# A four-layer graph network on one core: the seam between the LSTM and the first dense layer re-ordered

## The chip, the cores and the metric

The kernel runs on one core of a Trainium2 chip. A core has five engines, each with its own queue of instructions: PE (matrix multiply, with a weight loader shown as PEld), DVE (vector), ACT (activation functions), POOL (general SIMD) and SP (issues DMA transfers). Matmul results land in PSUM[...]. The metric is the device time of one execution in microseconds; the median of three runs is compared.

## The reference

Activations are x, [128 graphs, 64 nodes, 256 channels] in f32: 8192 tokens. Four layers follow each other, each as `x = x + layer(relu(layernorm(x)))`.

```
layer 0:  h = relu(adj @ (h @ Wg0 + bg0));  h = relu(adj @ (h @ Wg1 + bg1))
          for p in 1..4:  windows of p nodes -> LSTM over the p steps (weights of p),
                          the last hidden state replaces node p-1 of each window
layer 1:  h = A_hat @ h;  h = relu(batchnorm(h @ W1.T + b1));  batchnorm(h @ W2.T + b2)
layer 2:  a 3-way graph convolution with the diagonal, upper and lower part of adj
layer 3:  one attention head with a causal mask, then @ Wo
```

W1 is 512x256, so layer 1's first dense product makes 512 channels from 256. Its batch norm needs the mean and variance over all 8192 tokens before anything after it can go on.

## The kernel before, in words

Tokens are worked on in 16 supertiles `s` of 512 tokens. Most products use one level of Strassen: seven products in place of eight, with sums of weight blocks made in advance (`weight_sum`, four per weight, on POOL) and sums of data blocks made as they are needed. The code never lets a scheduler choose: each operation is recorded with a planned time through `at(...)`, the list is sorted by that time, and each engine gets its instructions in that order. The planned times only set the order. [...]

**Layer 0, graph part** (`graph_part`, `ROUND`): one supertile per round. Beside it POOL makes the summed LSTM weights of p = 2..4, six pieces per round (`stage`), and stores them in DRAM.

**LSTM** (`first_step`, `outer_step`): a step for one state is 52 slots of PE work. A slot is one 128x512 matmul or two 128x256 ones; each f32 matmul shows as two records in the trace, so 4 records of 128x256 or 2 of 128x512 are one slot. After the last slot comes a tail off PE: DVE adds the last banks to the gates (`chained` L1007, `take` L980), ACT applies the gates (`act` L1013), POOL computes `in_times_g` (L1023) and `plus` (L1029), with `keep` (L1026) before, ACT takes the tanh of the cell (`squash` L1032), and DVE multiplies with the output gate (`out` L1038). `n` is one of two halves of the data. In the very last step (`fin`) the POOL part goes by channel halves.

**Seam** (`begin`, `First`): while the last LSTM step runs, the first supertiles of layer 1 are prepared. For each: PE transposes the LSTM result (`turn` L666), ACT copies it out of PSUM (`turned` L670), POOL adds it to x (`added` L674), DVE takes layer norm statistics (`stats` L685, L686), POOL takes the root (`root` L692, L693), ACT normalises (`relu` L699), PE multiplies with the adjacency (`agg` L708), and ACT or DVE copies that to SBUF (`agged` L712). W1 is loaded in four transfers (`load_w1` L146) and its four sums are made on POOL (L314) in this stretch.

**First dense product** (`half`, `GATE`): supertiles go in pairs `i`, output channels in two halves `g`. One `half(i, g)` has seven products (L1290) into three banks:

```
c = (c,2)                              one product
b = (b,5) then (b,3)
a = (a,1), (a,6), (a,7), (a,4)         evicted between the steps
```

(a,1) is read by ACT (`evict` L1295) before (a,6) may add to the same bank. DVE adds the other banks to the evicted blocks (`add` L1298) and takes batch norm statistics (L1301). The data sums t1, t2, b12, t4 (`ag_sums` L1191) are made by DVE for pair 0 and by POOL for most others. At the start of this product the eight LSTM banks are closed and two new pools opened: `new_banks(gates=5, rest=3)`.

Of the kernel before, what the change touches and what calls it, by code (L numbers as in the profile page):

```python
# [14 lines left out]
P = 128  # L15
# [5 lines left out]
def kernel(ctx: ExitStack, tc: tile.TileContext, a: dict, out: bass.AP):  # L21
# [120 lines left out]
    def load_w1():  # L142
        con["w1"] = hlast.tile([P, 7, 2, P], F32, tag="w1", name="w1")
        for o in range(2):
            for c in range(2):
                nc.sync.dma_start(con["w1"][:, 2 * o + c], a["W1T"].rearrange(  # L146
                    "(c p) (g o m) -> o c p g m", c=2, p=P, o=2, m=P)[o, c])
# [182 lines left out]
    def pairs_of(p):  # L330
# [5 lines left out]
        if nblk % 2 == 0 and nw % nblk == 0:  # L336
# [8 lines left out]
              for p in range(2, NL + 1) for n, size in SUMS.items()}  # L345
    ORDER = (0, 2, 3, 1)
# [65 lines left out]
    with tc.tile_pool(name="pa", bufs=2) as pa, tc.tile_pool(name="pax", bufs=3) as pax:  # L412
# [189 lines left out]
        START = (9.01, 11, 19.01)  # L602
# [6 lines left out]
        at_piece = 3  # L609
# [38 lines left out]
    class First:  # L648
# [9 lines left out]
        def turn(self, k):  # L658
            v = self.v
            if k == 0:  # L660
                tag = "ag" if self.s == 3 else "h"
                v["h"] = pb[0].tile([P, Q, D], F32, tag=tag, name=tag)
            v["T", k] = bank(self.pool).rearrange("p (q d) -> p q d", q=2)
            for q in range(2):
                for c in range(KC):
                    nc.tensor.transpose(v["T", k][:, q, ts(c, P)], tile_rows(self.s, c, 2 * k + q), ident)  # L666

        def turned(self, k):

            nc.scalar.copy(self.v["h"][:, slice(2 * k, 2 * k + 2)], self.v["T", k])  # L670

        def added(self, k):
            v, qs = self.v, slice(2 * k, 2 * k + 2)
            nc.gpsimd.tensor_add(v["xt"][:, qs], v["xt"][:, qs], v["h"][:, qs])  # L674
# [20 lines left out]
        def relu(self, q):  # L695
            v = self.v
            if self.s == 3 and q == 0:
# [230 lines left out]
    def outer_step(t0, st, j, tags, fin):  # L928
# [105 lines left out]
        def out(n):  # L1034
            m = ("21", "22")[n]
            if last:
                for c in range(KC):
                    nc.vector.tensor_mul(x(n, c), wide(gate_(m, 0)[:, c]), wide(gate_(m, 1)[:, c]))  # L1038
# [21 lines left out]
        for c in range(KC):  # L1060
            tick((-26 if one else -38) + 0.6 * c, T1, c)
        for k, s in ((0, -35), (1, -34), (3, -33)):
            tick(s + 12 * one, inner_sum, 5, k)
# [41 lines left out]
        for c in range(KC if fin else 1):  # L1105
            c = slice(c, c + 1) if fin else slice(0, KC)
            tick(e, in_times_g, 1, c)
            tick(e, plus, 1, c)
        tick(58.5, out, 0)
        tick(e + (6.5 if last and p < NL else 4.2), squash, 1)  # L1110
        tick(e + (8.8 if last and p < NL else 6), out, 1)
        st["h_at"] = t0 + e + 6
# [68 lines left out]

    def ag_sums(i, k, engine=nc.gpsimd):
# [3 lines left out]
        if k == 0:  # L1186
            if i == 0:
                t = sums_of.tile([P, 3, 512], F32, tag="th", name="T")
                firsts[0]["t"] = [t[:, n, :] for n in range(3)]
# [3 lines left out]
    def begin(s, t_load, t_turn=None, t_stats=None, t_relu=None, t_agg=None):  # L1193
# [11 lines left out]
        def agg(c):  # L1205
            f.agg(c)
            f.agged(c, nc.vector.tensor_copy if s else nc.scalar.copy)
# [10 lines left out]
        if t_stats and s != 3:  # L1218
# [5 lines left out]
    begin(2, 7.9, 20.3, 21.4, 25.3)  # L1224
    begin(3, 17, 24.3, 25.4)
    begin(4, 21.4)
    at(t + 34.6, load_w1)
    for k in range(4):
        at(t + 48 + 0.1 * k, lambda k=k: weight_sum(con["w1"], k))
    at(t + 52.2, lambda: seam.extend(("a0", "a1", "c", "b")))  # L1230
    at(t + 68, lambda: First(3).root())
    for k in range(4):
        at(t + 57.4 + 0.1 * k, ag_sums, 0, k, nc.vector)
# [24 lines left out]
    with tc.tile_pool(name="pz", bufs=1, reuse_waits="tile") as pz:  # L1258
# [11 lines left out]
        new_banks(gates=5, rest=3)  # L1270
        GATE = 8.7
        B = GATE * (NS - 2)
# [5 lines left out]
        def half(i, g):  # L1278
            t0, r = GATE * (2 * i + g), {}
            z = {(n, o): zslot(2 * i + n, 2 * g + o) for n in range(2) for o in range(2)}  # L1280

            def product(name, j):
                new = name not in r
                if new:
                    r[name] = bank("gates")
                (b11, b21), (b12, b22) = ([firsts[2 * i + n]["ag"][:, c, :] for c in range(KC)]
                                          for n in range(2))
                t1, t2, t4 = firsts[0]["t"]
                x_ = (b11, b21, b22, t4, t1, t2, b12)[j - 1]
                nc.tensor.matmul(r[name], con["w1"][:, OF[j], g, :], x_, start=new,  # L1290
                                 stop=(name, j) in (("a", 4), ("b", 3), ("c", 2)), skip_group_check=True)

            def evict(n, o, name):
                m = 2 * g + o
                nc.scalar.activation(z[n, o], r[name], AF.Identity, bias=con["bn1"][:, 0, m : m + 1])  # L1295

            def add(n, o, name):
                nc.vector.tensor_add(z[n, o], z[n, o], r[name])  # L1298
# [5 lines left out]
            if end:  # L1304
                t0 = B + 6.02 * g
            late_a = 6.1 if g else 6.9
            for t, name, j in (((0, "c", 2), (1.72, "a", 1), (2.58, "b", 5), (3.44, "a", 6), (4.3, "b", 3),
# [3 lines left out]
                at(t0 + t, product, name, j)  # L1311
            for t, fn, n, o, name in (((2.6, evict, 0, 0, "a"), (3.3, add, 0, 0, "c"),
# [7 lines left out]
                at(t0 + t, fn, n, o, name)  # L1320
            for t, n, o in (((4.0, 0, 0), (7.3, 1, 0), (8.1 - 0.2 * g, 1, 1), (8.6, 0, 1)) if end else
                            ((5.5, 0, 0), (9.0, 1, 0), (9.7, 1, 1), (GATE + 2.9, 0, 1))):
                at(t0 + t, stats, n, o)
# [4 lines left out]
        for i in range(NS // 2):  # L1328
            for g in range(2):
                half(i, g)  # L1330
            for k, t in enumerate((-4.3, 0.9, 2.2, 3.5) if i else ()):
                at(GATE * 2 * i + t, ag_sums, i, k, nc.vector if i == NS // 2 - 1 else nc.gpsimd)
        for k in range(4):
            at(GATE * (4 + 2 * (k // 2)) + 9.7 + 0.8 * (k % 2), weight_sum, w2, k)
        for s in range(2, NS):
            f, t0 = First(s, "rest"), GATE * s
# [6 lines left out]
            if s <= 3:  # L1343
                continue
            if s > 4:
                at(t0 - 6 * GATE + 9.2, f.load)
            t1 = t0 - 4 * GATE
# [5 lines left out]
            for q in range(Q):  # L1353
                at(t2 + (1.7, 2.3, 4.2, 4.8)[q], f.stats, q)
            at(t2 + 5.4, f.root)

        tp, early = [], []

        def second_product(i):
# [39 lines left out]
            def product(name, j, ks=(0, 1)):  # L1399
                new = name not in banks  # L1400
                if new:
                    banks[name] = bank("gates" if i % 2 else "rest")
# [553 lines left out]
```

## Time and profile before

| | |
|---|---|
| median of 3 runs | 1832.97 us (1832.28 to 1833.19) |
| the profiled execution, its own time | 2696.76 us |
| its span, first to last instruction | 2695.0 us |
| granted PE clock in it | 0.655 of full speed, mean |
| busy in it: PE, PEld | 2680.4 us (99%), 1605.8 us |
| busy in it: DVE, ACT, POOL | 1198.1, 1006.6, 1178.5 us |
| bytes moved by DMA | 91.20 MB, 34 GB/s |

The profile and the timed runs are far apart: the profiled execution had the PE clock held at about two thirds. Durations on DVE, ACT, POOL and the DMA queues can be read from it as they are. Durations on PE are stretched, and waits of PE for the other engines are hidden by the stretching. The last LSTM matmul ends at about 1750.7 us of the span; the first dense product runs from 1753 us on.

### The profile page before, as it was taken

How to read it: one execution, taken by the hardware profiler on the slowest of the kernel's cores; microseconds unless marked ns; L12 is line 12 of the kernel's file. 1: busy time of each engine (PE TensorE's matmuls, PEld its weight loads, DVE VectorE, ACT ScalarE, POOL GpSimd, SP SyncE). 2: the span in 40 equal slices, each digit the busy share in tenths (PEclk: the TensorE clock that was granted, in tenths of full speed). 3: DMA queues.
4: the chain of work that ended last, by engine and by line, in shares of the span. 5: the costliest groups of instructions: out<-in, count | busy, mean ns of one | idle time of the engine just before them, and what ended most of it. 6: DMA issues, size and time to landing. Idle time of an engine off the chain costs nothing.

```text
span 2695.0 us, 24421 instructions
## 1 busy us (share of the span) xinstructions
PE 2680.4 (99%) x8532; PEld 1605.8 (60%) x8532; DVE 1198.1 (44%) x2346; ACT 1006.6 (37%) x1776; POOL 1178.5 (44%) x1207
## 2 busy tenths in 40 slices
PE   9999999999999999999999999999999999999999
PEld 7776333354354776677355555555433788888887
DVE  5543333343434444444344444465554444444443
ACT  4454444422423323333422222355453333323332
POOL 5654333443444444544434444554232444444442
PEclk7666666666666666666666666666666666666666
DMA  4344000000002000002000000222000000000000
GB/s 153 116 145 158 14 0 0 5 0 6 4 16 79 0 1 1 1 1 77 18 0 0 1 0 0 78 85 80 30 26 0 32 9 32 32 32 32 32 32 24
DMA packets 67498, 91.20 MB, mean 34 GB/s; under 512 B 4784, under 2 KB 57776, under 8 KB 67376
## 3 DMA queue, kind: packets, MB, share of 16 engines
q1 hardware_dynamic: 66928, 89.35, 9.9%
q8 instruction: 68, 1.11, 0.2%
q14 instruction: 54, 0.44, 0.1%
q10 hardware_dynamic: 448, 0.30, 0.0%
HBM read 56.08 MB, written 33.55 MB: 33 GB/s over the span
## 4 chain that ended last, share of the span: by engine, by line
PE 99%; DVE 0%; ACT 0%; DMA 0%; issue 0%; DVEq 0%
PE ps L969 21%; PE ps L993 18%; PE ps L861 17%; PE ps L1680 8%; PE ps L1290 5%; PE ps L1407 5%; PE ps L455 3%; PE ps L465 3%; PE ps L1767 3%; PE ps L1743 3%; PE ps L494 3%; PE ps L1647 2%; PE ps L1777 2%; PE ps L708 2%; PE ps L1808 2%; PE ps L666 1%
## 5 line engine op out<-in xcount | busy, mean ns | idle before, releaser
L980 DVE TENSOR_TENSOR gate<-gate,ps 128x512 f32<-128x512 f32 (+2 forms) x360 | 218.2, 606 | 444.1 <-PE ps L969 434.5
L1013 ACT ACTIVATE gate<-gate,lbias 128x512 f32<-128x512 f32 (+2 forms) x288 | 175.5, 651 | 278.7 <-DVE gate L1007 146.8
L874 DVE TENSOR_TENSOR gate<-gate,ps 128x512 f32<-128x512 f32 (+2 forms) x162 | 100.8, 645 | 268.0 <-PE ps L861 259.3
L978 ACT COPY gate<-ps 128x512 f32<-128x512 f32 (+2 forms) x144 | 75.0, 521 | 332.8 <-PE ps L969 332.7
L861 PE MATMUL ps<-tx,wih 128*128 128x512 f32 (+2 forms) x276 | 172.6, 760 | 0.0
L1680 PE MATMUL ps<-wl,ag 128*128 128x128 f32 x900 | 155.8, 348 | 0.0
L1680 PEld LDWEIGHTS ps<-wl,ag 128*128 128x128 f32 x900 | 150.3, 256 | 4.6 <-ACT ag L1652 2.6
L1023 POOL TENSOR_TENSOR gate<-gate 128x1024 f32<-128x1024 f32 (+3 forms) x37 | 73.3, 1982 | 181.8 <-ACT gate L1013 181.8
L969 PE MATMUL ps<-h,wb 128*128 128x256 f32 (+2 forms) x392 | 131.9, 475 | 0.7 <-ACT h L670 0.7
L969 PEld LDWEIGHTS ps<-h,wb 128*128 128x128 f32 x392 | 82.1, 211 | 84.4 <-issue 52.3
L877 ACT COPY gate<-ps 128x512 f32<-128x512 f32 (+2 forms) x108 | 59.7, 553 | 179.1 <-PE ps L861 177.4
L993 PE MATMUL ps<-hT,wb 128*128 128x512 f32 x160 | 119.5, 839 | 0.0
L861 PEld LDWEIGHTS ps<-tx,wih 128*128 128x128 f32 x276 | 58.6, 213 | 98.3 <-issue 84.9
L861 PE MATMUL ps<-hT,wih 128*128 128x512 f32 (+2 forms) x168 | 115.4, 806 | 0.0
L870 ACT ACTIVATE gate<-gate,lbias 128x512 f32<-128x512 f32 (+2 forms) x108 | 95.8, 887 | 50.8 <-DVE gate L874 50.6
L993 PE MATMUL ps<-wih,thA 128*128 128x512 f32 (+2 forms) x192 | 114.4, 688 | 0.0
L1623 ACT ACTIVATE h<-x,ln_rn 128x256 f32<-128x256 f32 x128 | 67.9, 592 | 111.5 <-POOL ln_rn L1620 111.5
L826 POOL TENSOR_TENSOR tx<-hT 128x512 f32<-128x512 f32 (+2 forms) x29 | 35.5, 1223 | 166.4 <-PE ps L861 154.7
L1007 DVE TENSOR_TENSOR gate<-gate,ps 128x512 f32<-128x512 f32 (+2 forms) x144 | 80.8, 603 | 54.4 <-PE ps L993 54.2
L861 PE MATMUL ps<-tx,wb 128*128 128x512 f32 x144 | 101.4, 838 | 0.0
L1026 POOL TENSOR_TENSOR cell<-cell,gate 128x1024 f32<-128x1024 f32 (+2 forms) x36 | 72.8, 2023 | 52.7 <-ACT gate L1013 52.7
L969 PEld LDWEIGHTS ps<-tx,wb 128*128 128x128 f32 x288 | 60.8, 215 | 58.5 <-issue 39.0
(333 smaller groups left out, 5828.8 us busy)
## 6 DMA issues: line engine op xcount, KB each, us to landing
xt<-in_x_dram SPq DMA_DIRECT2D x30, 512.0 KB, 4.0
x1d<-xt SPq DMA_DIRECT2D x16, 512.0 KB, 2.6
x<-x1d SPq DMA_DIRECT2D x16, 512.0 KB, 5.0
out_dram<-x SPq DMA_DIRECT2D x15, 512.0 KB, 2.9
W<-wb SPq DMA_DIRECT2D x6, 896.0 KB, 4.8
wb<-W SPq DMA_DIRECT2D x6, 896.0 KB, 4.5
wb<-in_WihT_dram SPq DMA_DIRECT2D x32, 128.0 KB, 3.4
wb<-in_WhhT_dram SPq DMA_DIRECT2D x24, 128.0 KB, 2.4
```

Source lines behind the costliest of these rows:

```text
L455: nc.tensor.matmul(p_[:, ts(q, P)], v[h][:, q, ts(c, P)], adjT_bd, start=True, stop=True)
L465: nc.tensor.matmul(p_[:, q, :], v["g0"][:, c, ts(2 * k + q, P)], con["wg0"][:, c, :], start=(c == 0), stop=(c == KC - 1))
L861: nc.tensor.matmul(wide(p_[:, :N]), wih_of(p, k, gi), x_, start=first_, stop=True, skip_group_check=True)
L870: nc.scalar.activation(to, r[bank_][:, :N] if bank_ else to, fn, bias=lbias[:, l, m : m + 1])
L874: nc.vector.tensor_add(slot(n, hc), slot(n, hc), r[bank_][:, :N])
L969: nc.tensor.matmul(B[pr, name][:, g * H : (g + 1) * H], w[:, g, :], d, start=(new and g == 0), stop=(name, k) in (("a", 4), ("b", 3), ("c" ...
L980: nc.vector.tensor_add(to, to, v)
L993: nc.tensor.matmul(to, w, d, start=(pr == 1 and c == 0), stop=(c == 1), skip_group_check=True)
L1013: nc.scalar.activation(v, v, FN[r, g], bias=lbias[:, l, b : b + 1])
L1290: nc.tensor.matmul(r[name], con["w1"][:, OF[j], g, :], x_, start=new, stop=(name, j) in (("a", 4), ("b", 3), ("c", 2)), skip_group_check=True)
L1407: nc.tensor.matmul(banks[name], w2[:, OF[j], k, :], x_, start=(new and k == 0), stop=(k == 1), skip_group_check=True)
L1680: nc.tensor.matmul(v["g", name][:, p_, :], x_[:, m, ts(p_, P)], wl2[:, OF[j], m, :], start=new and p_ == m == 0, stop=m == 2 and (name, j) ...
```

## The change

- **W1 sums staged.** W1 is loaded into the scratch tile `wcf` at the beginning, its four sums are made there in the first free POOL pieces, and the result is stored in DRAM. The LSTM weight pieces move back by one piece. At the seam one transfer fetches W1 with its sums.
- **Seam.** Supertile 3 is added to x by DVE straight from PSUM; its two blocks of transposes and its statistics come after the LSTM's last matmul. One transpose block of supertile 2 moves half a slot ahead.
- **First sums from PSUM.** For pair 0 the sums t1, t2 and b12 are made on DVE with one operand read from the PSUM bank of `agg`; supertile 1 needs one copy in place of two. t4 is made later.
- **Early eviction.** For the first block, DVE evicts bank a after (a,1); ACT's eviction for it is gone. The first four products of `half(0, 0)` are recorded in the LSTM's list, the other three come after the first two of `half(0, 1)`.
- **Banks.** The LSTM's eight banks stay open: products rotate over c, k0, k1, k2, b, the rest over the a's and k3, and the second dense product takes its banks from a table.
- **Statistics.** The batch norm statistics of the first gates come up to 8 planned us later.
- **LSTM.** In the last step of a group POOL's `in_times_g` and `plus` for n = 1 go by channel half; the last `squash` and `out` of steps with N < 512 come later in the order; sums of product 5 come later. In the very last step POOL, not DVE, makes the output of n = 1.

```diff
     def load_w1():
         con["w1"] = hlast.tile([P, 7, 2, P], F32, tag="w1", name="w1")
-        for o in range(2):
-            for c in range(2):
-                nc.sync.dma_start(con["w1"][:, 2 * o + c], a["W1T"].rearrange(
-                    "(c p) (g o m) -> o c p g m", c=2, p=P, o=2, m=P)[o, c])
+        nc.sync.dma_start(con["w1"], summed["w1"].rearrange("p (k g m) -> p k g m", k=7, m=P))
...
+    summed["w1"] = dram.tile([P, 1792], F32, tag="w1_d", name="w1_d")
...
-        START = (9.01, 11, 19.01)
+        START = (11, 16, 19.01)
...
+        w1 = wcf.rearrange("p (k g m) -> p k g m", k=7, m=P)
+
+        def load_raw_w1():
+            for o in range(2):
+                for c in range(2):
+                    nc.sync.dma_start(w1[:, 2 * o + c], a["W1T"].rearrange(
+                        "(c p) (g o m) -> o c p g m", c=2, p=P, o=2, m=P)[o, c])
+
+        events.append((9.01, len(events), load_raw_w1, ()))
+        for k in range(4):
+            stage(k, lambda k=k: weight_sum(w1, k))
+        stage(5, lambda: nc.sync.dma_start(summed["w1"], wcf))
+        at_piece = 4
...
         def turned(self, k):
 
-            nc.scalar.copy(self.v["h"][:, slice(2 * k, 2 * k + 2)], self.v["T", k])
+            v, qs = self.v, slice(2 * k, 2 * k + 2)
+            if self.s == 3:
+                nc.vector.tensor_add(v["xt"][:, qs], v["xt"][:, qs], v["T", k])
+            else:
+                nc.scalar.copy(v["h"][:, qs], v["T", k])
 
         def added(self, k):
             v, qs = self.v, slice(2 * k, 2 * k + 2)
-            nc.gpsimd.tensor_add(v["xt"][:, qs], v["xt"][:, qs], v["h"][:, qs])
+            if self.s != 3:
+                nc.gpsimd.tensor_add(v["xt"][:, qs], v["xt"][:, qs], v["h"][:, qs])
...
+                    (nc.gpsimd if fin and n else nc.vector).tensor_mul(x(n, c), wide(gate_(m, 0)[:, c]), wide(gate_(m, 1)[:, c]))
...
-            tick((-26 if one else -38) + 0.6 * c, T1, c)
-        for k, s in ((0, -35), (1, -34), (3, -33)):
-            tick(s + 12 * one, inner_sum, 5, k)
+            tick(-26 + 0.6 * c if one else -30.5 + 1.6 * c, T1, c)
+        for k, s in ((0, -23 if one else -28), (1, -22), (3, -21)):
+            tick(s, inner_sum, 5, k)
...
+        halves = fin or last and st["s"] == 0
+        for c in range(KC if halves else 1):
+            c = slice(c, c + 1) if halves else slice(0, KC)
             tick(e, in_times_g, 1, c)
             tick(e, plus, 1, c)
-        tick(58.5, out, 0)
-        tick(e + (6.5 if last and p < NL else 4.2), squash, 1)
-        tick(e + (8.8 if last and p < NL else 6), out, 1)
-        st["h_at"] = t0 + e + 6
+        tick(61 if fin else 58.5, out, 0)
+        squashed, done = (6.5, 8.8) if last and p < NL else (5, 8) if N < 512 else (4.2, 6)
+        tick(e + squashed, squash, 1)
+        tick(e + done, out, 1)
+        st["h_at"] = t0 + e + done
...
+    gates_order = ["c", "k0", "k1", "k2", "b"]
+
+    def gates_bank():
+        gates_order.append(gates_order.pop(0))
+        return bank(gates_order[-1])
+
+    def half_product(r, i, g, name, j):
+        new = name not in r
+        if new:
+            r[name] = gates_bank()
         (b11, b21), (b12, b22) = ([firsts[2 * i + n]["ag"][:, c, :] for c in range(KC)]
                                   for n in range(2))
-        if k == 0:
-            if i == 0:
-                t = sums_of.tile([P, 3, 512], F32, tag="th", name="T")
-                firsts[0]["t"] = [t[:, n, :] for n in range(3)]
+        t1, t2, t4 = firsts[0].get("t", [None] * 3)
+        x_ = (b11, b21, b22, t4, t1, t2, b12)[j - 1]
+        nc.tensor.matmul(r[name], con["w1"][:, OF[j], g, :], x_, start=new,
+                         stop=(name, j) in (("a", 4), ("b", 3), ("c", 2)), skip_group_check=True)
...
             f.agg(c)
-            f.agged(c, nc.vector.tensor_copy if s else nc.scalar.copy)
+            if s == 0:
+                f.agged(c)
...
-    begin(2, 7.9, 20.3, 21.4, 25.3)
-    begin(3, 17, 24.3, 25.4)
+    begin(2, 7.9, 19.85, 21.4, 25.3)
+    begin(3, 17, 28.75)
     begin(4, 21.4)
     at(t + 34.6, load_w1)
-    for k in range(4):
-        at(t + 48 + 0.1 * k, lambda k=k: weight_sum(con["w1"], k))
-    at(t + 52.2, lambda: seam.extend(("a0", "a1", "c", "b")))
-    at(t + 68, lambda: First(3).root())
-    for k in range(4):
-        at(t + 57.4 + 0.1 * k, ag_sums, 0, k, nc.vector)
+    at(t + 52.2, lambda: seam.extend((f"a{1 - turn_['a']}", f"a{turn_['a']}", "k3")))
+    def first_ag_sums():
+        b12, b22 = (firsts[1]["p", c] for c in range(KC))
+        b11, to = firsts[0]["ag"][:, 0, :], firsts[1]["ag"]
+        t = sums_of.tile([P, 3, 512], F32, tag="th", name="T")
+        t1, t2, _ = firsts[0]["t"] = [t[:, n, :] for n in range(3)]
+        nc.vector.tensor_sub(t1, b12, b11)
+        nc.vector.tensor_copy(to[:, 1, :], b22)
+        nc.vector.tensor_sub(t2, b22, t1)
+        nc.vector.tensor_sub(to[:, 0, :], to[:, 1, :], b12)
+
+    at(t + 57.4, first_ag_sums)
+    r00 = {}
+    for s, name, j in ((57, "c", 2), (57.1, "a", 1), (57.6, "b", 5), (57.7, "a", 6)):
+        at(t + s, half_product, r00, 0, 0, name, j)
+    at(t + 57.45, lambda: nc.vector.tensor_scalar_add(firsts[0]["t"][2], r00["a"], con["bn1"][:, 0, 0:1]))
...
-        new_banks(gates=5, rest=3)
         GATE = 8.7
+        LAG = 8.0
...
+                begun = firsts[0]["t"][2] if early and (n, o) == (0, 0) else z[n, o]
+                nc.vector.tensor_add(z[n, o], begun, r[name])
...
+            soon = {}
+            if early:
+                soon = {("b", 3): 5.6, ("a", 7): 5.7, (evict, 1, 1, "b"): 1.0, (evict, 1, 0, "a"): 1.1,
+                        (add, 0, 0, "c"): -2, (add, 1, 0, "b"): 5.75, (add, 1, 1, "a"): 5.8}
+            elif i == 0:
+                soon = {("c", 2): -3.4, ("a", 1): -3.3, ("b", 5): 0, ("a", 6): 0.8, (evict, 0, 0, "a"): -2.0,
+                        (add, 0, 0, "c"): -0.1}
...
+                at(t0 + t + max(0, LAG - 1.4 * (2 * i + g)), stats, n, o)
...
+        SECOND_BANKS = ((2, 0, 1), (1, 0, 2), (2, 1, 0), (3, 4, 1), (2, 0, 1), (2, 0, 3), (2, 1, 0), (1, 4, 2))
```

## The prediction

> **What bounds the kernel now.** First the page's engine table, clock row and chain.
>
> ```profile
> PE 2680.4 (99%) x8532; PEld 1605.8 (60%) x8532; DVE 1198.1 (44%) x2346; ACT 1006.6 (37%) x1776; POOL 1178.5 (44%) x1207
> ...
> PEclk7666666666666666666666666666666666666666
> ...
> PE 99%; DVE 0%; ACT 0%; DMA 0%; issue 0%; DVEq 0%
> ```
>
> PE bounds it at every stage of this execution, but its clock was held at 0.655 and it took 2696.76 us, 1.471 times the median of 1832.97. At full clock the same PE work is 2680.4 x 0.655 = 1756 us. I take the timed runs to be at full clock (my choice: the clock alone, without waits, would need 0.655 x 1.471 = 0.963). Then some 77 us of a timed run are PE waits and overheads, and the trace shows only about 15 (2695.0 - 2680.4). The rest is hidden: PE was slowed, the others not. So I read stages by asking what each engine has to do in PE's time x 0.655. The view by stretches, with PE, PEld, DVE, ACT and POOL busy in turn:
>
> ```profile
> 1728.00:1750.50 22.50, 21.75 (x68) 13.27 (x69) 11.44 (x26) 9.88 (x19) 17.12 (x15) 0.65 0.14 52
> 1750.50:1765.00 14.50, 13.48 (x47) 7.97 (x46) 12.81 (x22) 11.45 (x19) 9.22 (x8) 0.65 0.32 103
> 1765.00:1778.50 13.50, 13.50 (x43) 7.38 (x42) 7.29 (x18) 7.04 (x12) 5.17 (x6) 0.65 0.22 78
> ```
>
> The first row is the end of the LSTM: PE needs 21.75 x 0.655 = 14.2 us, POOL 17.12. POOL is the bound there. In the second, the seam, PE needs 8.8, DVE 12.8, ACT 11.5. In the third, two halves into the dense product, PE needs 8.8, DVE 7.3: PE leads again. So at full clock the seam is not PE's. The timeline of PE across it (start, length):
>
> ```profile
> 1749.23 1.46 PE L993 MATMUL ps<-gate,wb 128*128 128x512 f32 x2
> 1750.53 2.82 PE L708 MATMUL ps<-ahT,h 128*128 128x128 f32 x16
> 1753.12 2.82 PE L1290 MATMUL ps<-ag,w 128*128 128x512 f32 x4
> 1755.77 1.46 PE L708 MATMUL ps<-ahT,h 128*128 128x128 f32 x8
> 1757.07 1.45 PE L1290 MATMUL ps<-T,w 128*128 128x512 f32 x2
> 1759.55 1.46 PE L1290 MATMUL ps<-T,w 128*128 128x512 f32 x2 [1.02 <-issue]
> ```
>
> The last row is (a,6), with a wait of 1.02 us. The timelines of ACT and POOL say what it waits for:
>
> ```profile
> 1757.82 1.06 ACT L1032 ACTIVATE gate<-cell 128x1024 f32<-128x1024 f32 x1 [1.88 <-POOL cell L1029]
> 1758.78 0.67 ACT L1295 ACTIVATE hS<-ps,bn 128x512 f32<-128x512 f32 x1
> ...
> 1735.78 2.37 POOL L1026 TENSOR_TENSOR cell<-cell,gate 128x1024 f32<-128x1024 f32 x1 [2.25 <-ACT gate L1013]
> ...
> 1745.33 2.90 POOL L314 TENSOR_TENSOR w<-w 128x256 f32<-128x256 f32 x4
> ...
> 1754.45 1.65 POOL L1023 TENSOR_TENSOR gate<-gate 128x512 f32<-128x512 f32 x1 [0.19 <-ACT gate L1013]
> 1756.19 1.60 POOL L1029 TENSOR_TENSOR cell<-cell,gate 128x512 f32<-128x512 f32 x1
> ```
>
> (a,6) needs bank a evicted (L1295). That sits in ACT's queue behind the LSTM's last squash (L1032), which waits for POOL.
>
> [...] the eviction starts as the squash ends, 3 us after (a,1). [...]
>
> ```profile
> 1754.30 0.68 DVE L1191 TENSOR_TENSOR T<-ag 128x512 f32<-128x512 f32 x1
> 1755.01 1.65 DVE L1191 TENSOR_TENSOR T<-ag,T 128x512 f32<-128x512 f32 x1
> ```
>
> 0.68 us free, 1.65 beside POOL's 1.65. [...]
>
> **The change part by part**, at full clock, in us from E, the end of the last LSTM matmul. A slot of PE is 1.29 in the trace, 0.85 at full clock. Other durations are the trace's.
>
> *(a,6) before.* PE: two agg of supertile 1 (1.7), (c,2) and (a,1) (1.7), agg (0.85), (b,5) (0.85): it reaches (a,6) at E+5.1. POOL: the matmul that lets the first keep start ended at 1734.2, that is 16.5 before 1750.7; less 0.68 of wait, x 0.655, plus the wait, 11.0. DVE and ACT took 1.7 (1734.2 to 1735.8), so POOL starts at E-9.3. Its queue: keep, plus, keep 2.37+2.35+2.35, root 1.02+0.20, an addition of supertile 3 1.26, W1 sums 2.90, the other addition 1.27, the first half of the tail 1.28+1.27: 16.3, to E+7.0. ACT has had the second half's gates ready since E+3.8. Then 1.65+1.60 POOL, 1.06 squash, 0.67 eviction: E+12.0. **Stall 6.9 us**, where the slow trace has 1.02. If POOL were in time: 3.8+3.25+1.06+0.67 = 8.8, stall 3.7; if it starts 2 later, 8.9. These are the bounds.
>
> *(a,6) after.* POOL loses 2.90 and 2.53 of its queue, ACT the eviction. DVE's queue after E: last gate additions 0.13+1.28, supertile 3's addition 0.65, t1, copy, t2, b12 4 x 0.67, eviction 0.65: E+5.4. The sums take 0.67 each, not 1.65, because one operand is in PSUM. PE, with two half-slot transposes now here, gets to (a,6) at 5.1. Stall 0.4 (0 to 2). Gain 6.5.
>
> *Bank waits.* Twice in the last LSTM step PE waits 0.68 for ACT to empty a bank just filled by transposes (L670, at 1728.07 and 1740.72). That latency does not shrink with PE's clock. Moving a block half a slot ahead, and supertile 3's behind the LSTM, puts 0.85 of matmul between. Gain 1.4 (0.7 to 1.4).
>
> *What is late next.* (b,3) and (a,7) need evictions that are still behind the squash. POOL, 5.4 lighter, is now in time: 3.85+3.25+1.06, evictions at E+8.8 and 9.5; with (c,2), (a,1) of the next half put before them PE comes at 9.8 and 10.6. Cost 0, cover 0.3 to 1.1. But supertile 3's statistics are now behind all this on DVE: 5.4, addition 0.65, two outputs 1.2 (3.3 beside POOL), addition 0.68, four statistics 2.4, small ones 0.33: E+10.7 to 12.8; POOL's root 1.2; ACT's relus, which hold ACT's queue, some 2.7: E+14.6 to 16.7. PE wants that agg at 14.9. The additions that release (a,4), and t4, follow on DVE: to about 15, wanted at 14.1. Cost 1.5 (0 to 3).
>
> *Statistics put back.* Four of 0.69 per half leave DVE's way at the seam and return as 8 us shrinking by 1.4 per half, where DVE has 8.8 - 7.3 = 1.5 free. Cost 0; without that room the wait would move to (a,4).
>
> *Banks.* The same five and three: 0 (-0.5 to +0.5). *One transfer* for four at the seam: issued 28 us ahead of need in the trace, 18 at full clock, an 896 KB transfer lands in 4.8: 0. *POOL's output of the last step*: supertiles that come much later: 0.
>
> *W1 sums in the graph part.* POOL gets 4 x 0.73 = 2.9, SP four issues (0.6 each) ahead of the LSTM weights and x of a later round, a store of 896 KB. A round is 15.03 in the trace, 9.8 at full clock, and POOL's work in one reaches 11.0 (the round from 95.55: 4 x 0.73, 1.01, 1.27, 5.08, 0.74). So POOL is near the bound there, and a piece more can hold PE through the data sums. But the pieces are added where the first round had only 2.33 of weight sums, and the queue ends in an LSTM stage with POOL at 14 to 19 of 50. I take +0.5 (-0.5 to +3).
>
> *LSTM group ends.* Two POOL operations of 2.35 become four of 1.28 (+0.4 of POOL, four groups); later squash and sums only keep ACT and POOL from waiting at the head of their queues. PE has no wait there in the trace, and its engines are some 70% used at full clock. 0 (-2 to +1).
>
> Sum: -6.5 - 1.4 + 1.5 + 0.5 = **-5.9: 1827.0 us** from the median. Against the profiled execution's own 2696.76 (span 2695.0, 1.8 around it), at the same held clock, only the shown waits go: 1.02 + 2 x 0.68 = 2.4, so 2694.4.
>
> **The rivals.**
>
> *Small gain.* The timed runs had a clock near 0.963 and few hidden waits, or the graph part takes the whole 2.9 and supertile 3 its 3. For: POOL's 11.0 in a 9.8 round; PE 99%. Against: the first two stretches, where POOL or DVE has more work than PE at anything near full clock. -6.5 - 1.4 + 3 + 2.9 = -2.0: 1831.
>
> *Slower: supertile 3 holds ACT.* Its first two statistics were over by E+2 before; now a chain of DVE, POOL and ACT follows the seam, and ACT's queue stands at the first relu with evictions behind it. My sum has its root done at about E+12. If it lands 5.9 us later, at E+18 (DVE's outputs waiting on squash and POOL, evictions feeding back into DVE), the whole gain is gone; that is the point from which it decides. At 9 us later, with the graph part's full 2.9, it is -5.9 + 9 + 2.4 = +5.5: 1838. Against: no link of the chain has that much work.
>
> *Larger gain.* POOL 2 us later before, and 2 us from the LSTM: 1823.
>
> **How the numbers follow.** A measurement can tell about 0.2%, 3.7 us. My forecast with its bounds 0.57, larger gain 0.15, small gain 0.17, slower 0.11. Nearly all of the first and the larger fall below 1829.3: 0.70 faster; 0.19 within; 0.11 slower. The range for 8 in 10 runs from 1820 (both larger effects and the -0.5's) to 1833.5, which takes in the small gain and leaves out the slower rival.
>
> **What would show it.** If the after profile has a high clock: PE from the last LSTM matmul to the tenth L1290 product without a wait above 1 us, and the agg of supertile 3 as the largest. At a held clock: the waits at L670 and of (a,6) gone. POOL's L314 on W1 in the first 30 us, followed by data sums on time. I am wrong if the stretch from E to the fourth half is not some 5 us shorter, or if the graph part grows by 2 us or more.

## The result, and the profile after

| | median, us | ratio to before | 95% interval |
|---|---|---|---|
| before | 1832.65 (1832.03 to 1833.19, 5 runs) | | |
| after | 1825.91 (1824.48 to 1826.36, 5 runs) | 0.9962 | 0.9951 to 0.9972 |

The change saves 6.7 us; 5.9 were predicted. The profile of before shown above was at a held clock and the one of after is at full clock, so the comparison below uses a second execution of the unchanged kernel that was at full clock (span 1832.3 us, clock 0.998). The engine table, clock row and chain of after:

```profile
PE 1800.3 (99%) x8532; PEld 1299.8 (71%) x8532; DVE 1179.4 (65%) x2346; ACT 988.5 (54%) x1773; POOL 1205.9 (66%) x1215
...
PEclk9999999999999999999999999999999999999999
...
PE 92%; POOL 3%; DVE 2%; ACT 2%; issue 2%; DMA 0%; POOLq 0%; DVEq 0%; ACTq 0%
```

PE still bounds the kernel. POOL, DVE and ACT stand in the chain that ended last, as they do in before's at full clock (PE 90%, POOL 4%, ACT 2%, DVE 1%); the 99% shown for the held clock came with the slowed PE. Which waits went is read from the list of PE's waits (line, what it waited for: us in all, times, longest; line numbers are those of the kernel that was run, so they differ between executions). At the seam before, from 1150 us on:

```profile
PE ps L1290 <- ACT hS L1295: 3.1, 1, 3.1
PE ps L708 <- DVE ag L712: 1.7, 1, 1.7
PE ps L708 <- DVE gate L980: 1.3, 1, 1.3
PE ps L969 <- ACT h L670: 0.7, 1, 0.7
PE ps L708 <- ACT ag L670: 0.7, 1, 0.7
```

and after, at the seam and, in its first line, in the graph part:

```profile
PE ps L492 <- DVE h L506: 2.8, 1, 2.8
...
PE ps L983 <- DVE gate L994: 0.8, 1, 0.8
...
PE ps L722 <- ACT h L713: 0.4, 1, 0.4
...
PE ps L1212 <- ACT z L1331: 0.4, 1, 0.4
```

At the seam 7.3 us of waits became 1.5. In the graph part there is a wait of 2.8 us that before did not have. The chain of events at the seam, PE's timeline of after (start, length; L1007 is the last LSTM matmul, so E is 1172.54 + 1.02 = 1173.56):

```profile
1172.54 1.02 PE L1007 MATMUL ps<-gate,wb 128*128 128x512 f32 x2
1173.39 0.61 PE L675 MATMUL ps<-ident,hT 128*128 128x128 f32 x4
1173.84 2.25 PE L722 MATMUL ps<-ahT,h 128*128 128x128 f32 x16
1175.93 1.88 PE L1212 MATMUL ps<-ag,w 128*128 128x512 f32 x4
1177.65 0.61 PE L675 MATMUL ps<-ident,hT 128*128 128x128 f32 x4
1178.10 1.88 PE L1212 MATMUL ps<-T,w 128*128 128x512 f32 x4
```

The last row is (b,5) and (a,6), back to back: (a,6) starts at 1178.96, E+5.4. The same product before, and what PE did next:

```profile
1185.73 2.05 PE L1290 MATMUL ps<-T,w 128*128 128x512 f32 x2 [3.07 <-ACT hS L1295]
1187.57 1.91 PE L666 MATMUL ps<-ident,hT 128*128 128x128 f32 x8
1189.28 3.11 PE L1290 MATMUL ps<-ag,w 128*128 128x512 f32 x4
```

With E = 1172.96 + 1.02 = 1173.98, it starts at E+11.75. The lengths hold a second thing: the two records of (a,6) take 2.05 us where after's four take 1.88, and eight transposes take 1.91 where after takes 1.06. PE came out of the wait at half clock. The view by stretches of before shows it (stretch, length, PE busy, granted clock, then DMA); counted as time at 0.50 among time at 1.00, its first three rows come to some 6.8 us at half clock:

```profile
1184.00:1186.00 2.00, 0.27 (x1) 0.73 0.19 60
1186.00:1190.00 4.00, 4.00 (x11) 0.50 0.01 2
1190.00:1192.00 2.00, 2.00 (x4) 0.56 0.00 0
1192.00:1196.00 4.00, 4.00 (x18) 1.00 0.40 155
```

**Where the time went, by stretch.** Two marks on PE cut each profiled execution in three: G, the start of the last matmul of the graph part (L513, L515 before), and M, the start of the last matmul of the weight wc in the last LSTM step (L1007, L993 before), some 20 us ahead of E. "Rest" is the span less M, that is, the seam and all behind it.

| profiled execution | G | M - G, LSTM | rest, with the seam |
|---|---|---|---|
| before | 171.9 | 980.4 | 680.0 |
| after | 176.1 | 977.6 | 670.9 |
| difference | +4.2 | -2.8 | -9.1 |

The sum is -7.7, the difference of the two spans; the medians differ by 6.7. So the total was predicted well and its parts were not: the seam gave more, the LSTM gave something where nothing was said, and the graph part took more. From E to the start of the fourth half before takes 36.53 us and after 29.35, which is 7.2 shorter.

These marks are steadier than the times of whole executions. Over the thirteen executions at full clock (these two and those of the experiments below), M - G is 977.6 to 977.8 in the ten with the LSTM edits and 980.3 to 980.5 in the three without. Where a kernel's times spread more than this, the clock after waits has a part in it; the last section returns to that.

### The profile page after: what moved, and what is told of

It is laid out like the page before. It is cut to its first block, busy times and chain, and to the rows that moved or that the text cites. A ratio compares the mean times of both kernels' runs of the same rounds, so it can differ in the third digit from the quotient of the medians.

```text
span 1824.6 us, 24389 instructions
## 1 busy us (share of the span) xinstructions
PE 1800.3 (99%) x8532; PEld 1299.8 (71%) x8532; DVE 1179.4 (65%) x2346; ACT 988.5 (54%) x1773; POOL 1205.9 (66%) x1215
## 4 chain that ended last, share of the span: by engine, by line
PE 92%; POOL 3%; DVE 2%; ACT 2%; issue 2%; DMA 0%; POOLq 0%; DVEq 0%; ACTq 0%
PE ps L983 20%; PE ps L1007 17%; PE ps L875 15%; PE ps L1730 8%; PE ps L1212 5%; PE ps L1457 4%; PE ps L1817 3%; PE ps L463 3%; PE ps L453 3%; PE ps L1697 3%; PE ps L1793 2%; PE ps L492 2%; PE ps L1827 2%; PE ps L1858 1%; PE ps L722 1%
## 5 line engine op out<-in xcount | busy, mean ns | idle before, releaser
L875 PE MATMUL ps<-tx,wih 128*128 128x512 f32 (+2 forms) x276 | 117.8, 544 | 1.9 <-ACT gate L891 1.4
L1730 PE MATMUL ps<-wl,ag 128*128 128x128 f32 x900 | 108.3, 276 | 0.6
L1730 PEld LDWEIGHTS ps<-wl,ag 128*128 128x128 f32 x900 | 104.2, 192 | 3.3 <-ACT ag L1702 2.5
L1037 POOL TENSOR_TENSOR gate<-gate 128x1024 f32<-128x1024 f32 (+4 forms) x41 | 73.8, 1800 | 42.1 <-ACT gate L1027 42.1
L983 PEld LDWEIGHTS ps<-h,wb 128*128 128x128 f32 x392 | 71.1, 190 | 39.6 <-issue 22.0
L983 PE MATMUL ps<-h,wb 128*128 128x256 f32 (+2 forms) x392 | 91.3, 355 | 0.0
L875 PEld LDWEIGHTS ps<-tx,wih 128*128 128x128 f32 x276 | 51.5, 190 | 55.6 <-issue 39.5
L922 POOL TENSOR_TENSOR cell<-gate 128x1024 f32<-128x1024 f32 (+2 forms) x36 | 78.1, 2192 | 5.4 <-ACT gate L884 5.4
L1007 PE MATMUL ps<-hT,wb 128*128 128x512 f32 x160 | 81.7, 592 | 0.0
L1007 PE MATMUL ps<-wih,thA 128*128 128x512 f32 (+2 forms) x192 | 79.3, 495 | 0.0
L875 PE MATMUL ps<-hT,wih 128*128 128x512 f32 (+2 forms) x168 | 78.5, 572 | 0.4 <-DVE h L499 0.4
L1043 POOL TENSOR_TENSOR cell<-cell,gate 128x1024 f32<-128x1024 f32 (+4 forms) x41 | 74.1, 1808 | 3.2
```

What stands on the lines that cost most here:

```text
L875: nc.tensor.matmul(wide(p_[:, :N]), wih_of(p, k, gi), x_, start=first_, stop=True, skip_group_check=True)
L922: nc.gpsimd.tensor_mul(cell[:, n, :, :N], i, g_)
L983: nc.tensor.matmul(B[pr, name][:, g * H : (g + 1) * H], w[:, g, :], d, start=(new and g == 0), stop=(name, k) in (("a", 4), ("b", 3), ("c" ...
L1007: nc.tensor.matmul(to, w, d, start=(pr == 1 and c == 0), stop=(c == 1), skip_group_check=True)
L1730: nc.tensor.matmul(v["g", name][:, p_, :], x_[:, m, ts(p_, P)], wl2[:, OF[j], m, :], start=new and p_ == m == 0, stop=m == 2 and (name, j) ...
```

## The experiments

**The kernel before, unchanged.** This is the full-clock execution used above (1834.04 us).

> The kernel before, unchanged, to see it at a high PE clock. Seam theory: PE waits 6.9 us at (a,6), its sixth block after the last LSTM matmul, and 0.7 twice in the last LSTM step; after it, from the end of the last LSTM matmul to the start of the fourth half, is some 6 us longer than in the changed kernel. LSTM theory: the waits at (a,6) are near 2 us and the LSTM stretch itself is 4 us or more longer than in the changed kernel.

The waits of 0.7 at L670 and the stall ahead of (a,6) are there. The stall is 6.0 us, in three waits on the way to (a,6) rather than in one: 1.26 and 1.66 for DVE, then 3.07 for the eviction. PE therefore reached (a,6) at E+8.7 and not at E+5.1. In both DVE waits DVE's queue stood at a statistic of supertile 3, which waited 1.99 and 1.16 us for POOL's addition.

**W1 at the seam again** (four raw transfers and four sums on POOL there; the staging in the graph part gone).

```diff
-        nc.sync.dma_start(con["w1"], summed["w1"].rearrange("p (k g m) -> p k g m", k=7, m=P))
+        for o in range(2):
+            for c in range(2):
+                nc.sync.dma_start(con["w1"][:, 2 * o + c], a["W1T"].rearrange(...)[o, c])
...
+        at(t + 48 + 0.1 * k, lambda k=k: weight_sum(con["w1"], k))
```

> The changed kernel with W1 loaded and its four sums made on POOL at the seam again. Seam theory: POOL has 2.9 us more before the tail of the LSTM, but was some 4 us early there for the first half of the tail, so (b,3) and (a,7) are delayed by 0 to 2 us; the graph part gets 0.5 back: +1 against the changed kernel, about 1827. Rival (the graph part pays for the staging): 2.5 us faster than the changed kernel, about 1823.5.

1823.23 us (1823.09 to 1823.79), ratio 0.9950 [0.9938, 0.9963]: 2.7 us faster than the changed kernel. G is 172.3, as before, and the rest 671.4, only 0.5 more than with staging. Here, staging costs more than it brings. All five times lie below all five of the changed kernel.

**The first eviction behind the squash, on ACT.**

```diff
-    at(t + 57.45, lambda: nc.vector.tensor_scalar_add(firsts[0]["t"][2], r00["a"], con["bn1"][:, 0, 0:1]))
+    at(t + 62, lambda: nc.scalar.activation(firsts[0]["t"][2], r00["a"], AF.Identity, bias=con["bn1"][:, 0, 0:1]))
```

((a,6) is recorded later with it, at t + 62.1.)

> The changed kernel with the first block of bank a evicted by ACT, recorded behind the LSTM's last squash as in the kernel before, and (a,6) after it. Seam theory: (a,6) waits until E + 8.6 + 0.7 = 9.3 where PE is there at 5.3: 4 us slower than the changed kernel, about 1830. Rival (the eviction's place is not what counts, POOL's lightening did it): within 1 us of the changed kernel.

1829.79 us (1826.45 to 1834.99, 21 runs), ratio 0.9986 [0.9979, 0.9992]: 3.9 slower than the change. ACT's timeline has the eviction where before had it:

```profile
1182.60 1.06 ACT L1046 ACTIVATE gate<-cell 128x1024 f32<-128x1024 f32 x1 [1.16 <-POOL cell L1043]
1183.56 0.67 ACT L1273 ACTIVATE T<-ps,bn 128x512 f32<-128x512 f32 x1
```

PE waits 3.67 us for it and then runs at half clock (0.50 in 1184 to 1188 us, 0.75 in 1188 to 1192). This profiled execution is near the long end of a wide spread (1833.89). By the median, the eviction's place alone is worth 3.9 us.

**The same on ACT, but at the early place** (t + 57.45, all else as changed).

> The changed kernel with the first eviction on ACT, but written at the early place, ahead of the last squash in ACT's queue. Order theory (behind the squash cost 3.9 us because of the queue, not because of ACT): the eviction is done near E+5.5, the squash is put off by at most 0.7 us; 1826 to 1826.6. Engine theory (ACT itself is slower or fuller here than DVE): 1828 or more, up to the 1829.8 of the kernel with the eviction behind the squash.

1827.15 us (1823.0 to 1828.15, 5 runs), ratio 0.9964 [0.9951, 0.9976]. This is between the theories. PE waits 1.46 us: ACT reaches the eviction at 1175.39, behind the first half's squash, and does it in 0.66, no slower than DVE's 0.74. In both kernels ACT took the two as they are written: the second half's squash at 1182.60 and the eviction at 1183.56 there, the eviction at 1175.39 and that squash at 1176.65 here. So it is the queue again, with a cost a little above the one expected: the rest is 672.1, 1.2 more than after, and the medians differ by 1.2 too. The profiled execution is the fastest of the five, 1823.0, because the wait in the graph part is missing from it (G is 171.5). That becomes important below.

**The first sums from SBUF copies.**

```diff
+        b12, b22 = (to[:, c, :] for c in range(KC))
+        for c in range(KC):
+            nc.vector.tensor_copy(to[:, c, :], firsts[1]["p", c])
-        nc.vector.tensor_copy(to[:, 1, :], b22)
```

> The changed kernel with the aggregated blocks of supertile 1 copied from PSUM to SBUF first (two DVE copies), and the three first sums made from the copies, as two-SBUF-operand operations. Port theory (the gain at the seam needs the PSUM operand: beside a busy POOL such a sum takes some 1.65 us, with a PSUM operand 0.68): one more copy 0.68 and up to three sums at +0.97, so the path to the fourth product is 2.6 to 3.6 us longer, and 1828.5 to 1829.5 comes out. Rival (only the place in the queue counts): one copy more, +0.7, 1826.6.

1828.60 us (1826.65 to 1832.36, 12 runs), ratio 0.9977 [0.9968, 0.9985]; 2.7 slower, as the first theory said; by the rest of the profile (673.0 for 670.9) it is 2.1. DVE's three sums in it:

```profile
1176.96 0.73 DVE L1266 TENSOR_TENSOR T<-ag 128x512 f32<-128x512 f32 x1
1177.72 1.66 DVE L1267 TENSOR_TENSOR T<-ag,T 128x512 f32<-128x512 f32 x1
1179.30 1.75 DVE L1268 TENSOR_TENSOR ag<-ag 128x512 f32<-128x512 f32 x1
```

The first, which began 0.25 us ahead of POOL's operation of 1.61, took 0.73; the other two, which began while POOL was at work, took 1.66 and 1.75. In the changed kernel the same sums, with one operand read from PSUM, take 0.68 each while POOL goes from one operation of 1.28 to the next. (a,6) waits 2.43 us for DVE. So the times with the PSUM operand, and of the two beside POOL without it, are near those that the prediction had put in (0.67 and 1.65).

**The LSTM edits undone** (T1, the sums of product 5, `halves`, `squashed`, `done` as before).

```diff
-        halves = fin or last and st["s"] == 0
+        halves = fin
-        squashed, done = (6.5, 8.8) if last and p < NL else (5, 8) if N < 512 else (4.2, 6)
+        squashed, done = (6.5, 8.8) if last and p < NL else (4.2, 6)
```

> The changed kernel with the LSTM edits undone (group ends whole, squash and output of short steps early, sums of product 5 early). Seam theory: within 1 us of the changed kernel, 1826 to 1827. LSTM theory: 3 us or more slower, 1829 or above.

1828.48 us (1824.19 to 1829.39, 6 runs), ratio 0.9973 [0.9962, 0.9985]: 2.6 slower. Two of its runs are as fast as the changed kernel's, so the stretch decides: M - G is 980.3, before's 980.4, after's 977.6. PE's waits for ACT's gate copies at L875 are 3.2 us (2.2 after), and two waits of 1.3 in all for POOL's sums of product 5 (L983 for L969) are back. That is 2.3 of the 2.7. Which of the edits removed which wait was not tried one by one.

**The statistics at their old place** (LAG = 0).

> The changed kernel with the statistics of the first halves of the dense layer at their places of before (no delay). Seam theory: DVE has room, 0 within 0.5, 1825.9. Rival (DVE, now with three more PSUM operations at the seam, is short there, and the delay is what keeps the sums on time): up to the four statistics' 1.6 us later, 1827.5.

1826.37 us (1824.83 to 1826.97, 5 runs), ratio 0.9961 [0.9949, 0.9974]: 0.5 slower, inside the seam theory's bound and less than the spread of either kernel. One new wait of 0.57 for t4 (DVE, L1220) shows where the delay helps; the rest is 671.2, 0.3 more than after.

**What costs in the graph part: one operation.** In the changed kernel, DVE, then POOL, then PE:

```profile
96.33 4.56 DVE L187 TENSOR_SCALAR dd<-ident,deg 128x128 f32<-128x128 f32 x1 [0.46 <-POOL deg L183]
```

```profile
96.28 2.49 POOL L369 TENSOR_TENSOR wb<-wc,wb 128x512 f32<-128x512 f32 x2
98.73 0.72 POOL L311 TENSOR_TENSOR wb<-wb 128x256 f32<-128x256 f32 x1
99.41 0.72 POOL L311 TENSOR_TENSOR wc<-wc 128x256 f32<-128x256 f32 x1
100.09 0.72 POOL L484 TENSOR_TENSOR t<-g 128x256 f32<-128x256 f32 x1
```

```profile
101.70 0.67 PE L492 MATMUL ps<-t,wg 128*128 128x256 f32 x2 [2.80 <-DVE h L506]
102.21 5.30 PE L463 MATMUL ps<-wg,g 128*128 128x256 f32 x16
```

The 128x128 operation begins 0.05 us after POOL's row of sums and ends as that row ends. PE waits for the DVE operation behind it. Its 16 matmuls after the wait take 5.30 us and not the 3.62 of an undisturbed round, since PE runs at half clock here too (0.65 in 102 to 104 us, 0.50 in 104 to 106). So 2.8 of wait cost 2.8 + 1.7 here. In the execution with the statistics at their old place the same wait is there, PE keeps its clock, and G is 174.4 for 176.1:

```profile
101.75 0.67 PE L492 MATMUL ps<-t,wg 128*128 128x256 f32 x2 [2.82 <-DVE h L506]
102.26 3.62 PE L463 MATMUL ps<-wg,g 128*128 128x256 f32 x16
```

The experiment puts that one operation on ACT and leaves all staging where it is:

```diff
-        nc.vector.tensor_scalar_mul(dd, ident, deg[:, 3:4])
+        nc.scalar.activation(dd, ident, AF.Identity, scale=deg[:, 3:4])
```

> The changed kernel with one 128x128 operation of the graph part (the diagonal of degrees) on ACT instead of DVE; all staging stays. In the trace of the changed kernel that operation begins on DVE at 96.33 us and takes 4.56 us, until the moment at which POOL's unbroken row of sums ends (100.8); with W1 summed at the seam it takes 1.30 us. Lock theory (the staging's cost in the graph part is this one DVE operation, kept out by POOL's row, which the four added slots have shifted against it): PE's wait of 2.8 us goes, time 1825.9 - 2.8 = 1823.1, although POOL still has all W1 sums. Load theory (POOL has 2.9 us of sums more than it had, and its data sums are late): the wait stays, 1825.9.

**1821.83 us** (1821.68 to 1822.23, 5 runs), ratio 0.9939 [0.9927, 0.9952]. It is 4.1 faster than the changed kernel, and the fastest kernel here. ACT's operation and the round behind it:

```profile
97.99 0.39 ACT L187 ACTIVATE dd<-ident,deg 128x128 f32<-128x128 f32 x1
```

```profile
99.64 3.62 PE L463 MATMUL ps<-wg,g 128*128 128x256 f32 x16
```

G is 171.8. The load theory falls: POOL has all of W1's sums and its data sums are in time. The lock theory was right that this operation carries the cost, and too low on the size, 2.8 for 4.1: it left out the half clock. A second witness is the execution above with the eviction on ACT at the early place. It has the graph part of the changed kernel unaltered, but the operation took 1.30 us on DVE, PE did not wait, and G is 171.5.

**Useless matmuls in before's wait.** Three go ahead of (a,6), into the bank that the next half's c then uses:

```diff
+                if (i, g, name, j) == (0, 0, "a", 6):
+                    kept.append(bank("gates"))
+                    for n in range(3):
+                        nc.tensor.matmul(kept[0], con["w1"][:, OF[1], g, :], firsts[0]["ag"][:, 0, :],
+                                         start=True, stop=True, skip_group_check=True)
```

> The kernel before, with three useless matmuls of 128x512 (0.86 us each, into the bank that the next half takes anyway) put on PE just ahead of (a,6), where PE waits for 3.07 us in its full-clock trace. After that wait PE runs at half clock for some 6 us, as the clock column shows. Clock theory (a wait of about 3 us costs its own length and then about as much again, since PE comes out of it at half clock): with 2.6 us of the wait filled PE keeps its clock, and the kernel is some 3 us faster for doing more work, 1830. Rival (only the length of the wait counts, the clock falls for another reason): 1832.8, or some tenths more.

In the profile the clock theory holds. PE's timeline, useless matmuls first, and the stretch behind them:

```profile
1182.46 2.74 PE L1290 MATMUL ps<-ag,w 128*128 128x512 f32 x6
1185.68 1.10 PE L1296 MATMUL ps<-T,w 128*128 128x512 f32 x2 [0.49 <-issue]
1186.62 1.06 PE L666 MATMUL ps<-ident,hT 128*128 128x128 f32 x8
```

```profile
1186.00:1188.00 2.00, 2.00 (x12) 1.00 0.01 3
1188.00:1190.00 2.00, 2.00 (x11) 1.00 0.00 0
```

(a,6) starts when it did, 1185.7, the clock stays at 1.00, and the rest is 677.2 against 680.0: 2.8 us won by keeping PE busy with nothing. The times are inconclusive: median 1831.28 (13 runs) against 1832.79 (19 runs), ratio 0.9995 [0.9986, 1.0003]. Before's own runs reach from 1830.8, with a mean clock of 1.0, to 1833.9, with 0.998, so not each of them has the whole 6.8 us at half clock. The clock itself agrees with the theory: its mean is 1.0 in 12 of the 13 runs with the useless matmuls and in 2 of the 19 without.

**Supertile 3 as before** (through ACT and POOL, statistics inside the LSTM; the diagonal on ACT, so 1821.83 is its base).

```diff
-    begin(3, 17, 28.75)
+    begin(3, 17, 24.3, 25.4)
+    at(t + 68, lambda: First(3).root())
```

(`turn`, `turned` and `added` are those of before again.)

> The changed kernel with the diagonal of degrees on ACT (1821.8 alone), and supertile 3 as before: transposes and statistics inside the last LSTM step, through ACT's copy and POOL's addition. Theory of the prediction: a bank wait of 0.7 us at the copy returns, what supertile 3 made late (0.4 + 0.4) goes; POOL's 2.5 us return into a gap of 2.4 us that its trace shows ahead of the tail, so nothing: 1821.5 to 1822. Rival (the 2.5 us of POOL are what made the tail late): squash and evictions 2.5 later, less a cover of about 1: 1823.3 or more.

1823.85 us (1823.4 to 1824.75, 5 runs), ratio 0.9953 [0.9941, 0.9966]: 2.0 slower, and the rest is 2.0 longer (673.0 for 671.0). The size is near the rival's, by another way than either said. No wait for the squash appears. PE waits 0.54 and 1.32 us for DVE's first sum and for its eviction, because supertile 3's four statistics stand ahead of them in DVE's queue, and 0.67 at the bank of `turned`. So moving supertile 3 away was worth 2 us through DVE.

**Both back, W1's sums too**, so that POOL has its whole queue of before.

> As the kernel with supertile 3 put back and the diagonal on ACT, and W1's four sums on POOL at the seam too, so that POOL has its whole queue of before there, while the first eviction is DVE's. Theory of the prediction (POOL's queue sets the last squash; with all 5.4 us back, less the gap of 2.4, squash and the evictions behind it are 3 us later, past the cover of 0.3 to 1.1): 2 to 3 us on PE at (b,3), half clock after it perhaps: 1824 to 1826. Rival (with the eviction on DVE nobody waits for POOL any more): 1821.5 to 1822.

1827.58 us (1826.67 to 1828.76, 7 runs), ratio 0.9973 [0.9962, 0.9984], slower than either expected. Again DVE, not the squash, is late:

```profile
1174.15 0.43 DVE L686 BATCH_NORM_STATS2 ln_st<-xt 128x6 f32<-128x256 f32 x1 [1.17 <-POOL xt L675]
...
1175.24 0.69 DVE L1254 TENSOR_TENSOR T<-ps,ag 128x512 f32<-128x512 f32 x1
```

```profile
1176.08 1.10 PE L1199 MATMUL ps<-T,w 128*128 128x512 f32 x2 [1.89 <-DVE T L1254]
1178.53 2.04 PE L1199 MATMUL ps<-T,w 128*128 128x512 f32 x2 [1.35 <-DVE T L1263]
```

W1's sums (2.91 on POOL) hold supertile 3's second addition; its statistic waits for that at the head of DVE's queue, with the first sums of the dense layer behind it. After two waits 1.1 us apart PE is at half clock: two records take 2.04 us where the two ahead of the second wait took 1.10. The two parts of the change that unload POOL are worth 5.8 us together (1827.58 - 1821.83), half clock included. Alone, supertile 3's is worth 2.0, and W1's, by the rest of the span with W1 at the seam, 0.5. So their gains do not add up one by one.

**W1 at the seam, diagonal and root on ACT.** The wait of 0.8 at L983 in the changed kernel follows a root's DVE operation of 128x4 that takes 2.22 us beside POOL's 2.35. This kernel gives ACT the two such operations of supertiles 0 and 1.

```diff
+                nc.scalar.activation(v["rn"][:, 0, :], v["mv"][:, :, 1], AF.Identity, bias=eps[:, 0:1])
+                nc.scalar.mul(v["rn"][:, 1, :], v["mv"][:, :, 0], -1.0)
```

> The changed kernel with W1 loaded and summed at the seam again, the diagonal of degrees on ACT, and the two 128x4 operations of the layer norm root of supertiles 0 and 1 on ACT instead of DVE. In the trace of the changed kernel one of these takes 2.22 us on DVE beside POOL's 2.35, and a wait of 0.76 us of PE for a gate sum behind it follows. Lock theory: both locks are gone, 1821.8 (the kernel with the diagonal on ACT) - 0.8 = 1821.0. Rival (the gate sum would be late anyway, or ACT, which has these operations now, is late): 1821.8 to 1823.

1823.51 us (1822.65 to 1823.84, 5 runs), ratio 0.9949 [0.9935, 0.9963]: no gain over W1 at the seam alone (1823.23). The wait of 0.8, which W1 at the seam alone still has, is gone, so the root's operation on DVE was its cause. But PE waits 1.62 us for the evictions behind the squash instead:

```profile
1180.07 1.96 PE L1206 MATMUL ps<-ag,w 128*128 128x512 f32 x4 [1.62 <-ACT hS L1327]
```

POOL's first operation of the tail starts right behind W1's sums (1169.64 to 1172.52), with no gap, and POOL's row is at the same times as with W1 at the seam alone. PE, now earlier, only waits longer for it. This is the (b,3) wait that the prediction had put at 0 for a POOL without these sums. Root on ACT together with staging was not tried.

## Why the prediction was right or wrong, point by point

The total was right, 5.9 for 6.7. That is in part luck: two terms came out better than said, by 2.7 and 2.8 us, and one worse, by 3.7, which takes most of that back.

- **(a,6)**: right. Before at E+12.0, measured 11.75; after at E+5.4, measured 5.4. POOL's first keep at E-9.3, measured 1164.34, E-9.6; its second half at E+7.0, measured 1180.59, E+6.6. The estimate from a held clock, other engines' durations kept and PE's scaled, held: the squash took 1.06 us at 0.655 and 1.06 after, four records of L1290 2.82 at 0.655 and, scaled, 1.85, where after takes 1.88. The stall was put at one place and is three waits; the two for DVE (2.9 us) were not foreseen, but they lie ahead of the eviction and so do not move its end. That POOL is now "in time" for the squash held too: evictions at 1182.1 to 1183.35, E+8.5 to 9.8, no wait at (b,3).
- **Missing term at the seam: the clock after a wait.** The sum took a stall at its length. In the profiled execution before's stall of 3.07 also cost 2.8 at half clock, as the useless matmuls showed. The seam gave 9.1 where -6.5 - 1.4 + 1.5 = -6.4 was said: waits 7.33 - 1.54 = 5.8, clock 2.8, and 0.5 not attributed. The timed executions of before have on average a higher clock (0.998 to 1.0 in 19 runs) than the profiled one (0.998), which fits the medians' 6.7 for the profiles' 7.7. By the prediction's own mark, some 5 us less from E to the fourth half, the seam was right (7.2).
- **Bank waits**: both of 0.67 (0.68 in the execution at 0.655) are gone, as predicted. A new one of 0.76 stands just ahead of the last LSTM matmul (L983, behind the root's operation of 2.22 us on DVE), which no step named.
- **What is late next, 1.5**: supertile 3's relu 0.41 and the eviction behind it 0.37. Right in kind, 0.8 in size.
- **W1 sums in the graph part, +0.5 (-0.5 to +3)**: the failed step. It cost 4.2 in the profiled execution and 4.1 by the timed experiment, outside its bounds; 2.6 of this is the wait and the rest the half clock. It was argued from POOL's load, which was harmless. What cost was one small DVE operation, which took 4.56 us beside POOL's row of sums (96.28 to 100.81 us). With the staging PE's wait of 2.8 us is there in five of the six profiled executions that have the operation on DVE, without it in none of three. Why is not shown: with W1 at the seam, too, the operation begins 0.06 us behind the start of an unbroken POOL row (96.53 for 96.47), and takes 1.30. By the prediction's own mark, a graph part 2 us longer, this part was wrong.
- **LSTM group ends, 0 (-2 to +1)**: mis-sized, and outside the bounds. They gave 2.8 in the profile and 2.6 timed. "PE has no wait there" was read from an execution whose slow PE hid waits, the effect that the same text had warned of for the seam.
- **Statistics**: 0, measured 0.3 in the profile and 0.5 timed (the delay helps a little, if at all). **Banks**, **one transfer**, **POOL's last output**: 0; no run isolates them, and what is left at the seam is 0.5.
- **The rivals**: the slower one needed supertile 3's root at E+18. POOL began it at 1185.27, E+11.7, and was done at E+13.5, where the prediction had about 12. Of the small gain's reasons the graph part came true and more (4.2 for 2.9); supertile 3 (0.8 for 3) and a clock near 0.963 (0.998 to 1.0) did not. Of the larger gain's, the 2 us from the LSTM came true (2.8); POOL was not later before (E+6.6 for 7.0).

## What to carry to other kernels

Read a wait on the bounding engine with what follows it: here the matmuls behind one and the same wait of 2.8 us cost nothing, 1.7 or some 3 us more, and the clock column says which. When a small operation of one engine runs beside a long row of another, look at its longest time and not at its size: here 4.56 us for one of 128x128 and 2.22 for one of 128x4. Moving it to another engine (ACT took 0.39) was worth more here than lightening POOL's load: 4.1 us against 2.7 for taking the staging out. Do not take "no wait" from an execution in which the bounding engine was slowed.

## What was not expected of the hardware

**The same wait can cost clock or not.** PE's wait of 2.8 us at L492 is there in five profiled executions, and their graph parts differ by up to 3.2 us:

| execution | mean granted clock, whole execution | G |
|---|---|---|
| statistics at their old place | 1.000 | 174.4 |
| after | 0.999 | 176.1 |
| LSTM edits undone | 0.999 | 176.0 |
| first sums from SBUF copies | 0.999 | 176.3 |
| eviction behind the squash (half clock at the seam, too) | 0.996 | 177.6 |

The first two in the view by stretches:

```profile
97.38:100.79 3.41, 1.55 (x14) 1.00 0.33 133
100.79:104.20 3.41, 2.45 (x11) 1.00 0.73 294
```

```profile
99.18:102.60 3.42, 0.90 (x4) 1.00 0.88 359
102.60:106.01 3.41, 3.41 (x9) 0.50 0.17 68
```

In the first the clock stays at 1.00, in the second it is at 0.50 for 3.41 us. At the seam it fell to 0.50 in before (wait 3.07), with the eviction behind the squash (3.67) and with both parts back (1.89 and 1.35). It did not fall there with the first eviction on ACT at the early place (1.46), with W1 at the seam and diagonal and root on ACT (1.62), with the first sums from SBUF copies (2.43) and with supertile 3 as before (0.54 and 1.32). So the length of a wait does not tell alone: 2.8 us left the clock at 1.00 in one execution and not in another. What decides is not shown here. The times of one kernel step with the clock: the kernel with the first sums from SBUF copies has 1826.65 to 1827.24 at a mean clock of 1.0, 1828.57 to 1828.69 at 0.999, 1830.02 to 1830.33 at 0.998 and 1832.36 at 0.997. The kernel with the diagonal on ACT, which has no such wait, hardly spreads (1821.68 to 1822.23).

**One DVE operation of 128x128 took 4.56 us in one execution and 1.30 in another**, beside the same order of POOL operations. The second is the execution with the eviction on ACT at the early place:

```profile
96.51 1.30 DVE L187 TENSOR_SCALAR dd<-ident,deg 128x128 f32<-128x128 f32 x1 [0.44 <-POOL deg L183]
```

There it began 0.10 us behind the start of POOL's row (96.41) and ended at 97.81, about half way through the row's first two operations (2.53 us); in the changed kernel it began 0.05 us behind and ended at 100.89, with the row (100.81). What decides between the two is open.
